# Attention and non-local block in one kernel: score blocks and value products in runs of six instead of four

## Chip, cores and metric

One Trainium2 chip, one core. The metric is the device time of one execution in microseconds (us), taken over several runs of each kernel. TensorE is the matmul engine, ScalarE applies functions (here the exponential) and copies, VectorE adds and inverts, GpSimd does a few multiplications. In the profile they are called PE (with PEld for its weight loads), ACT, DVE and POOL.

## The reference, cut to what matters

Eight images of 512 channels and 32 x 32 positions pass through an attention layer with eight heads of 64 channels, then through a non-local block and a normalization over the batch. All is fp32. The change touches only the middle three lines:

```
q, k, v = 1x1 convolutions of x          # (8, 8 heads, 64, 1024)
attn = softmax(einsum('bhdn,bhdm->bhnm', q, k) * 64**-0.5, axis=-1)
out  = einsum('bhnm,bhdm->bhdn', attn, v)
x    = x + conv1x1(out)
# theta, phi, g; f = theta phi^T / n; y = f g; z = conv1x1(y) + x; normalize z over the batch
```

## The kernel before

For one image the scores are cut into 64 blocks: 4 pairs of heads `p`, 2 halves `h` of the 1024 query positions, 8 stretches `m` of 128 key positions. A *score block* is the product of 128 keys with 512 queries for both heads of a pair (`ps`), which ScalarE turns into exponentials `e`. A *value product* multiplies `e` of one block with the values and adds it to `po`; eight of them make one *sum*, for one `(p, h)`. VectorE meanwhile adds the eight `e` to `acc`; the matrix product of ones and `acc` (`psum`, the *row-sum product*) gives the softmax's denominator, which VectorE inverts. TensorE writes scores with two heads as two row tiles (64*128) and value and row-sum products with two heads as two column tiles (128*64); going from one shape to the other costs time, and so the kernel works in runs: `RUN` score blocks, then `RUN` value products of the run before. In the code below, cuts are marked `...` and the comments are added.

```python
    RUN = 4
    ...
    w2 = ctx.enter_context(tc.tile_pool(name="w2", bufs=2))               # acc, ri
    ring = ctx.enter_context(tc.tile_pool(name="ring", bufs=12))          # e blocks
    psS = ctx.enter_context(tc.tile_pool(name="psS", bufs=1, space=PSUM)) # 3 tags x 2 banks: scores
    psO = ctx.enter_context(tc.tile_pool(name="psO", bufs=2, space=PSUM)) # 2 banks: po and psum
    ...
    def attention(b, q, k, v, before_last):
        o = mats.tile([P, CC, N], F32, tag="o", name=f"o_{b}")
        steps = [(p, h, m) for p in range(NPAIR) for h in range(NH) for m in range(NB)]
        runs = [steps[i:i + RUN] for i in range(0, len(steps), RUN)]
        ...
        def normalize(p, h, lead):
            s = slice(h * 512, (h + 1) * 512)
            ps = psO.tile([P, 512], F32, tag="o", name=f"psum_{b}_{p}_{h}")
            acc = accs.pop((p, h))
            columns(ps, lambda j: ones, lambda j: acc[:, j, :], True, True, lead)
            ri = w2.tile([P, 512], F32, tag="ri", name=f"ri_{b}_{p}_{h}")
            nc.vector.reciprocal(ri, ps)
            nc.vector.tensor_tensor(o[:, p, s], o[:, p, s], ri, ALU.mult)

        def weighted(run, due):
            lead = True
            if due:
                normalize(*due.pop(), True)
                lead = False
            for p, h, m in run:
                if m == 0:
                    sums[p, h] = psO.tile([P, 512], F32, tag="o", name=f"po_{b}_{p}_{h}")
                ps, e = sums[p, h], es.pop((p, h, m))
                columns(ps, lambda j: v[:, m, (2 * p + j) * D:(2 * p + j + 1) * D], lambda j: e[:, j, :],
                        m == 0, m == NB - 1, lead)
                lead = False
                if m == NB - 1:
                    nc.scalar.copy(o[:, p, h * 512:(h + 1) * 512], sums.pop((p, h)))
                    due.append((p, h))

        due = []
        for i, run in enumerate(runs):
            scores(run)
            if i:
                weighted(runs[i - 1], due)
        before_last()                  # q of the next image
        weighted(runs[-1], due)
        normalize(*due.pop(), False)
        return o
```

PSUM is the memory in which this kernel puts its matmul results, in tiles of one bank, 512 columns, or two. `po` and `psum` share the two banks of `psO`; six more banks (`psS`) hold scores. `columns` issues the two column tiles; its `lead` form splits the very first product of a value run. TensorE's order is the program's order.

## Time and profile before

| | before |
|---|---|
| median of 3 runs (us) | 2346.35 (2342.19 to 2347.3) |
| span of the profiled run (us), mean granted clock | 2342.2, 0.982 |
| busy share: TensorE, VectorE, ScalarE | 96%, 60%, 30% |
| value runs in an image | 16 |
| score run of 4 blocks, value run of 4 products, the same with a row-sum product (us) | 3.63, 3.59, 4.45 |

The last row is read from start to start: from the first matmul of one run to the first of the next. The main lines of this profile stand in the prediction below. TensorE's timeline at the end of the second image's attention (start, length, instruction, count), where the last row-sum product follows the last value products and the next image's value projection follows that:

```profile
543.60 2.75 PE L289 MATMUL po<-e,v 128*64 128x512 f32 x12
546.17 1.03 PE L289 MATMUL psum<-acc,ones 128*64 128x512 f32 x4
547.13 3.72 PE L171 MATMUL pv<-w_WvT,x 128*128 128x256 f32 x16
```

A length in this view reaches past the start of the next row (543.60 + 2.75 is 546.35, and the next row starts at 546.17); the starts count.

### The profile page before, as it was taken

To read this page: it belongs to the slowest core of one execution; us is meant where nothing else is said; L and a number is where in the kernel's file an instruction comes from. 1 tells how busy PE (TensorE), PEld (TensorE's weight loads), DVE (VectorE), ACT (ScalarE), POOL (GpSimd) and SP (SyncE) were. 2 spreads that over 40 slices of the span, in tenths; PEclk is the share of its full clock that TensorE was granted. 3 is DMA by queue.
4 is the path that set the end of the run, shared out by engine and by line. 5 is a ranking of instruction groups with operands and counts; after the bars stand their busy time and mean duration, and the time that the engine had idled before them with its cause. 6 is when DMAs were issued, how large, how long until landed. Compare 5 with 4: busy or idle time off the path is not lost.

```text
span 2342.2 us, 20797 instructions
## 1 busy us (share of the span) xinstructions
PE 2240.7 (96%) x8562; PEld 1127.6 (48%) x8562; DVE 1397.7 (60%) x1261; ACT 704.4 (30%) x819; POOL 61.7 (3%) x56
## 2 busy tenths in 40 slices
PE   4999999999999999999999999999999999999990
PEld 1533655336643466434563355633655346643360
DVE  2277445783567744687348854488445773477745
ACT  0155102541035310453104521154202541035205
POOL 2000110000000000000000000000000000000000
PEclk7999999999999999999999999999999999999995
DMA  6000122001130021200121002210113001200327
GB/s 233 1 1 7 64 85 108 28 1 63 47 135 1 1 76 66 104 1 32 48 94 72 1 32 76 90 48 1 63 47 135 1 1 63 79 16 1 108 86 310
DMA packets 30950, 141.94 MB, mean 61 GB/s; under 512 B 4096, under 2 KB 10496, under 8 KB 26112
## 3 DMA queue, kind: packets, MB, share of 16 engines
q1 hardware_dynamic: 26000, 131.87, 15.2%
q10 hardware_dynamic: 4848, 8.67, 1.0%
q8 instruction: 69, 1.13, 0.2%
q14 instruction: 33, 0.27, 0.0%
HBM read 101.07 MB, written 39.45 MB: 60 GB/s over the span
## 4 chain that ended last, share of the span: by engine, by line
PE 94%; ACT 2%; DVE 1%; DMA 1%; POOL 0%; issue 0%; ACTq 0%; DVEq 0%; POOLq 0%
PE ps L270 20%; PE po L289 17%; PE pv L171 8%; PE ptp L171 8%; PE pk L171 8%; PE pp L171 8%; PE pq L171 8%; PE pg L171 4%; PE pz L171 4%; PE pf L359 2%; PE psum L289 1%; PE pwf L378 1%; ACT z L504 1%; PE po L287 1%; PE po L286 1%; PE psum L287 1%
## 5 line engine op out<-in xcount | busy, mean ns | idle before, releaser
L273 ACT ACTIVATE e<-ps 128x1024 f32<-128x1024 f32 x512 | 482.5, 1030 | 360.3 <-PE ps L270 360.3
L279 DVE TENSOR_TENSOR acc<-acc,e 128x1024 f32<-128x1024 f32 x384 | 467.4, 1217 | 164.0 <-ACT e L273 135.7
L270 PE MATMUL ps<-q,k 64*128 64x512 f32 x2048 | 473.3, 603 | 1.6 <-POOL q L256 1.6
L289 PE MATMUL po<-e,v 128*64 128x512 f32 x1904 | 464.3, 594 | 0.0
L270 PEld LDWEIGHTS ps<-q,k 64*128 64x128 f32 x2048 | 187.6, 187 | 284.2 <-issue 233.6
L289 PEld LDWEIGHTS po<-e,v 128*64 128x64 f32 x1904 | 153.3, 137 | 211.9 <-issue 200.7
L297 DVE RECIPROCAL ri<-psum 128x512 f32<-128x512 f32 x64 | 214.5, 3352 | 10.2 <-PE psum L289 10.2
L368 ACT ACTIVATE g<-pg,gb 128x512 f32<-128x512 f32 x32 | 22.0, 687 | 428.6 <-PE pg L171 428.6
L171 PE MATMUL pq<-t_x,w_WqT 128*128 128x512 f32 x256 | 117.8, 608 | 26.0 <-ACT q L228 21.1
L188 DVE TENSOR_TENSOR k<-k,pk 128x1024 f32<-128x1024 f32 x24 | 29.3, 1221 | 163.1 <-PE pk L171 163.1
L171 PE MATMUL pp<-t_o,w_WpT 128*128 128x512 f32 x256 | 116.3, 602 | 1.9 <-DVE x L331 1.9
L171 PE MATMUL ptp<-w_tp,t_x 128*128 128x256 f32 x512 | 114.4, 379 | 0.0
L171 PE MATMUL pv<-w_WvT,t_x 128*128 128x256 f32 x512 | 114.4, 379 | 0.0
L171 PE MATMUL pk<-t_x,w_WkT 128*128 128x512 f32 x256 | 113.8, 592 | 0.0
L171 PEld LDWEIGHTS ptp<-w_tp,t_x 128*128 128x128 f32 x512 | 97.3, 190 | 13.2
L171 PEld LDWEIGHTS pv<-w_WvT,t_x 128*128 128x128 f32 x512 | 97.3, 190 | 13.2
L228 ACT ACTIVATE q<-pq,bq 128x512 f32<-128x512 f32 x64 | 40.4, 684 | 182.8 <-PE pq L171 182.8
L171 PE MATMUL pq<-x,w_WqT 128*128 128x512 f32 x192 | 88.7, 605 | 5.3 <-DMA w_WqT<-in_WqT_dram 5.3
L171 PEld LDWEIGHTS pq<-t_x,w_WqT 128*128 128x128 f32 x256 | 49.9, 196 | 90.1 <-issue 62.4
L188 DVE TENSOR_TENSOR q<-q,pq 128x1024 f32<-128x1024 f32 x24 | 29.3, 1221 | 102.1 <-PE pq L171 102.1
L277 DVE TENSOR_TENSOR acc<-e,e 128x1024 f32<-128x1024 f32 x64 | 78.3, 1223 | 16.6 <-ACT e L273 15.7
L171 PE MATMUL pp<-o,w_WpT 128*128 128x512 f32 x192 | 88.2, 603 | 0.0
(117 smaller groups left out, 2193.2 us busy)
## 6 DMA issues: line engine op xcount, KB each, us to landing
x<-in_x_dram SPq DMA_DIRECT2D x32, 512.0 KB, 5.5
w_WpT<-kept_WpT SPq DMA_DIRECT2D x7, 1792.0 KB, 7.1
w_tp<-kept_tp SPq DMA_DIRECT2D x7, 1792.0 KB, 7.2
spill<-x SPq DMA_DIRECT2D x24, 512.0 KB, 3.8
z<-spill SPq DMA_DIRECT2D x24, 512.0 KB, 8.4
out_dram<-z SPq DMA_DIRECT2D x24, 512.0 KB, 6.0
w_WqT<-kept_WqT SPq DMA_DIRECT2D x6, 1792.0 KB, 7.4
w_WvT<-kept_WvT SPq DMA_DIRECT2D x6, 1792.0 KB, 7.0
```

Of the source, the lines that this page charges most:

```text
L171: pe(nc.tensor.matmul(to_ps, lhsT(k), rhs(k), start=(s, at) not in begun, stop=(k == nk - 1), skip_group_check=True))
L188: nc.vector.tensor_tensor(at, at, ps, ALU.add)
L228: nc.scalar.activation(t[:, c, cols(q)], ps[:, m, :], AF.Identity, bias=bias[:, c:c + 1])
L270: pe(nc.tensor.matmul(ps[:, j, :], k[r, p, m * P:(m + 1) * P], q[r, p, h * 512:(h + 1) * 512], start=True, stop=True))
L273: nc.scalar.activation(e, ps, AF.Exp, scale=SCALE)
L277: nc.vector.tensor_tensor(accs[p, h], es[p, h, 0], e, ALU.add)
L279: nc.vector.tensor_tensor(accs[p, h], accs[p, h], e, ALU.add)
L286: pe(nc.tensor.matmul(to[:, :LEAD], l, r[:, :LEAD], start=start, stop=False, skip_group_check=True))
L287: pe(nc.tensor.matmul(to[:, LEAD:], l, r[:, LEAD:], start=False, stop=stop, skip_group_check=True))
L289: pe(nc.tensor.matmul(to, l, r, start=start, stop=stop, skip_group_check=True))
L297: nc.vector.reciprocal(ri, ps)
L359: pe(nc.tensor.matmul(ps[:, c, :], tp[:, i, c * P:(c + 1) * P], tp[:, i, CI:], start=(i == 0), stop=(i == NB - 1)))
```

## The change

Fewer changes between the two shapes: 11 value runs an image instead of 16. Twelve buffers for `e` hold exactly two runs of six.

```diff
-    RUN = 4
+    RUN = 6
```

## The prediction

> **What bounds the kernel now.** I read four views, in this order: the page (busy shares and chain), the groups by line, the timeline of single engines over the attention of the second image, and the waits of the matmul engine.
>
> The page first. The columns are busy time, share of the span and number of instructions; below it stands the chain that ended last.
>
> ```profile
> PE   2240.7 (96%) x8562; PEld 1127.6 (48%) x8562; DVE 1397.7 (60%) x1261; ACT 704.4 (30%) x819; POOL 61.7 (3%) x56
> ...
> PE 94%; ACT 2%; DVE 1%; DMA 1%; POOL 0%; issue 0%; ACTq 0%; DVEq 0%; POOLq 0%
> PE ps L270 20%; PE po L289 17%; PE pv L171 8%; PE ptp L171 8%; PE pk L171 8%; PE pp L171 8%; PE pq L171 8%; PE pg L171 4%; PE pz L171 4%; PE pf L359 2%; PE psum L289 1%; PE pwf L378 1%; ACT z L504 1%; PE po L287 1%; PE po L286 1%; PE psum L287 1%
> ```
>
> TensorE is the bound: it is on the chain for 94% of the span, and scores (L270) with value products (L286 to L289) are some 40% of it. Nothing else comes near, so a change counts only by the time in which TensorE issues no matmul, or issues one late. The groups (busy us, mean ns, then idle before) give the companions of one score block:
>
> ```profile
> L273 ACT ACTIVATE e<-ps 128x1024 f32<-128x1024 f32 x512 | 482.5, 1030 | 360.3 <-PE ps L270 360.3
> L279 DVE TENSOR_TENSOR acc<-acc,e 128x1024 f32<-128x1024 f32 x384 | 467.4, 1217 | 164.0 <-ACT e L273 135.7
> L297 DVE RECIPROCAL ri<-psum 128x512 f32<-128x512 f32 x64 | 214.5, 3352 | 10.2 <-PE psum L289 10.2
> ```
>
> The timeline, TensorE and ScalarE rows of one run of four score blocks and one of four value products (start, length, instruction):
>
> ```profile
> 411.29 3.70 PE L270 MATMUL ps<-q,k 64*128 64x512 f32 x16
> ...
> 414.93 0.32 PE L286 MATMUL po<-e,v 128*64 128x128 f32 x1
> ...
> 415.84 2.75 PE L289 MATMUL po<-e,v 128*64 128x512 f32 x12
> ...
> 418.52 1.56 PE L270 MATMUL ps<-q,k 64*128 64x512 f32 x6
> 418.63 0.59 ACT L313 COPY o<-po 128x512 f32<-128x512 f32 x1 [2.39 <-PE po L289]
> ```
>
> The reader is to see that one period of scores and values (411.29 to 418.52) is 7.23 us without any idle entry on PE, and that the copy of a finished `po` (ScalarE, L313) runs beside the next scores, so it costs nothing. The first score run holds two runs back to back:
>
> ```profile
> 400.63 7.14 PE L270 MATMUL ps<-q,k 64*128 64x512 f32 x32
> ```
>
> It lasts 7.07 us from its start to the first value product at 407.70; 16 matmul records last 3.64 us (411.29 to 414.93). So 16 more records cost 3.43 us, 0.86 us a block, and entering the run costs 3.64 - 3.43 = 0.21. A value run takes 418.52 - 414.93 = 3.59 us for the same 3.43 of work: 0.16 for entering. **One pair of changes costs 0.21 + 0.16, or 7.23 - 6.87 = about 0.355 us** with the unrounded starts. The waits of the matmul engine in the whole kernel show no wait inside attention, but one wait of the kind that matters below, TensorE for a ScalarE copy that it follows at once:
>
> ```profile
> PE pz L171 <- ACT wf L380: 9.3, 8, 1.2
> ```
>
> **What the Trainium skill says.** "TensorEngine Tiling (Array Packing)", Key Properties: changing the tiling mode, not just the tile, drains TensorE. The trace agrees: score records (64*128) and value records (128*64) start in pairs 0.43 us apart, and 0.53 us across each change. It is what the change wants to save. "PSUM — Partial Sum Buffer", the section on bank collisions: TensorE may not write a bank that another engine reads, and the semaphores must see to it; so a new `po` in a bank must wait until the copy or the reciprocal that reads it has ended. The trace before shows no collision and no such wait in attention. "TensorE: Matmul & The Clock Gate", the table at its head: ScalarE takes its queue strictly in order; so a copy also waits for the exponentials ahead of it. The copy above ran 0.11 us after the next scores began, with the exponentials long done. "Perfetto Trace Analysis", Tensor Engine Instruction: a matmul's end is estimated, not observed; I therefore count from start to start.
>
> **The change part by part.** One image has 4 head pairs x 2 halves x 8 = 64 blocks: 16 runs of four before, now ten of six and one of four. No instruction for a block is added or removed; the built order shows that only the 80 TensorE rows of the split lead products go.
>
> *Removed.* Value runs per image go from 16 to 11, so 5 pairs of changes go: 5 x 0.355 = 1.78 us an image, x 8 images = **-14.2 us**. All on the path, because TensorE is.
>
> *Moved: the products of the sums.* Before, a sum of eight products (`po`) always ended a run; its bank was copied out while four score blocks ran, and the row-sum product `psum` opened the next value run in the other of the two banks. With six, eight does not divide: sums end inside runs 1, 2, 5, 6 and 9 (counted from 0) and the next sum begins at once. It needs a bank. In runs 1, 5 and 9 the other bank is free (a reciprocal has read it; see below). But runs 2 and 6 open with a `psum`, which has taken the other bank, so the next `po` must take the bank of the `po` that ended one instruction earlier, and waits for its copy. The built program says so: the first product of po_1_0 and po_2_1 carries a wait on ScalarE, and both have the bank of the sum before. A third such wait stands at the end: the `psum` of the seventh sum has slipped behind the next image's q projection, into the last value run, and so the eighth `psum` gets the bank of the eighth `po`, just ended, with a wait on ScalarE. In the kernel before, none of the `po` products and no `psum` had a wait on ScalarE.
>
> *Cost of one such wait.* From the trace: the last pair of `po` starts at 417.99 and the copy at 418.63, 0.64 later; it takes 0.59; `pz` after the `wf` copy starts 0.05 after the copy's end. Without the wait the next pair would start 0.43 after the last. The restart after an empty array costs a further 0.10 (0.53 instead of 0.43, as at a change of mode). 0.64 + 0.59 + 0.05 - 0.43 + 0.10 = 0.95 us. Three an image, eight images: 3 x 8 x 0.95 = **+22.8 us**.
>
> *Added: twelve score blocks at the start.* ScalarE needs 0.92 us a block when busy (the 8 at 401.87 took 7.44: (7.44 - 1.03) / 7), TensorE 0.86, and three score buffers lie between. In the eight blocks of before, weights for the last block were loaded some 0.25 us ahead of its matmul; that lead shrinks by 0.06 a block, so the 12th block comes some 0.1 to 0.2 us late: 8 x 0.15 = **+1.2 us**. Runs of six begin with ScalarE idle and stay clear of it.
>
> *VectorE beside it.* With `psum` later by up to a run, the first addition into an `acc` buffer waits for the `psum` that reads its old content (two buffers), and reciprocals come later. I laid out one image by hand with 1.3 us an addition (3.88 us for three in the timeline) and 4.0 us for a reciprocal with its multiplication: VectorE idles twice (some 10 and 7 us), but ends each piece before TensorE needs it; the tightest are the banks of the third and sixth `psum`, read by the reciprocal 4 to 6 us before a `po` takes them, and the data sums of the next image, ready 2 to 3 us before use. Twelve block buffers hold exactly two runs of six; each is free 4 us or more before its exponential. So VectorE adds nothing by this count.
>
> Sum: -14.2 + 22.8 + 1.2 = **+9.8 us**, 2346.35 + 9.8 = **2356 us**.
>
> **The rivals.** (a) *Only the changes go.* If the waits for the copies were hidden (the copy starts earlier, or the matmul queue bridges them), the time would be 2346 - 14 = 2332. For: the changes are measured, 0.355 a pair. Against: nothing stands in TensorE's order between the last product and the next one into the same bank. I give it one in ten. (b) *VectorE becomes the bound.* It has 56 x 1.3 + 8 x 4 = 105 us in an image's attention of some 118 us, and now idles in the middle. If my hand layout is out by more than the 4 us of slack, a `po` waits for a reciprocal (3.35 us) once or twice an image: +8 x 2 to 5 = 2372 to 2396. For: 89% load and two long idle times. Against: each reciprocal starts as soon as its `psum` is there. One in ten. (c) *The end of the image suffers*: the seventh and eighth reciprocal now both follow the q projection, and the products of `o` must be ready for the output projection. Against: the value projection of 25 us lies between, except in the last image: at most +3 us.
>
> **Range and chances.** The three runs before spread over 5 us; the cost of a wait may be 0.7 to 1.1 us, which moves the sum by -6 to +4; rival (b) stretches the top, rival (a) the bottom. Range 2342 to 2368. A change of 2% is 47 us, more than any rival but the end of (b): faster 0.01, same 0.96, slower 0.03.
>
> **What would show it.** Right: TensorE's waits list `po` waiting for the ScalarE copy of L313, 16 times at about 0.65 to 0.9 us, and `psum` 8 times; six-block runs last 5.35 us of scores and 5.3 us of values, 80 changes fewer. Wrong: `po` waiting for the reciprocal (b), no wait at all (a), scores waiting for exponentials in runs of six, or q or v projections that start late. A time under 2342 would mean that the copies are hidden; one over 2368 that VectorE or the buffers of the blocks hold TensorE up.

## The result, and the profile after

| | before | after |
|---|---|---|
| median of 6 runs (us) | 2343.26 (2341.89 to 2347.3) | 2352.43 (2349.68 to 2353.0) |
| ratio to before, 95% interval | 1 | 1.0034 (1.0021 to 1.0047) |
| span of the profiled run (us), mean granted clock | 2342.2, 0.982 | 2350.8, 0.981 |
| all score runs, 8 images (us) | 465.0 | 458.7 |
| all value and row-sum runs, 8 images (us) | 514.7 | 529.2 |

A ratio here and below is the mean time of one kernel's fast runs over that of the other's of the same rounds, so it is not quite the ratio of the medians quoted. The last two rows add up, from matmul starts in the trace, the time from the first matmul of each run to the first of the next run. They contain every wait in it. The change lost 8.6 us in the traces, and these two stages account for 14.5 - 6.3 = 8.2 of them.

TensorE has less to do and takes longer. Its busy line on the page after:

```profile
PE 2234.9 (95%) x8482; PEld 1118.1 (48%) x8482; DVE 1388.8 (59%) x1261; ACT 699.8 (30%) x819; POOL 61.7 (3%) x56
```

Eighty matmul records and 5.8 us of busy time are gone, and yet the span grew. What TensorE waited for (us in total, times, longest):

```profile
PE po L289 <- ACT o L313: 10.9, 16, 0.7
PE pz L171 <- ACT wf L380: 9.3, 8, 1.2
PE psum L289 <- ACT o L313: 4.8, 7, 0.7
```

The line in the middle was there before. The first and third are new: value products and row-sum products that wait for the copy of a finished sum. TensorE's timeline of the value run in which it happens first in the second image:

```profile
434.57 0.32 PE L286 MATMUL psum<-acc,ones 128*64 128x128 f32 x1
...
435.48 3.60 PE L289 MATMUL po<-e,v 128*64 128x512 f32 x16
439.77 1.94 PE L289 MATMUL po<-e,v 128*64 128x512 f32 x8 [0.68 <-ACT o L313]
441.64 1.56 PE L270 MATMUL ps<-q,k 64*128 64x512 f32 x6
```

The run opens with the row-sum product of the first sum (L286), ends the second sum (16 records are four blocks), and the third sum begins at 439.77 only, after 0.68 us without a matmul. In the same run of the kernel before, this place did not exist: a sum ended a run. The chain of work that ended last shows that the copy itself lies on the path (start, length, what):

```profile
435.65 3.46 PE po L289 x16
439.11 0.02 issue
439.13 0.59 ACT o L313
439.73 0.04 issue
439.77 1.94 PE po L289 x8
```

The idle time understates the loss, because the modelled length of the last matmul reaches into the gap: eight pairs from 435.48, 0.43 apart, put the start of the last pair at 438.49, and the next pair starts 1.28 later, 0.85 more than usual. From start to start, this run took 441.64 - 434.57 = 7.07 us; a run of six with a row-sum product and no wait takes 6.17. So one wait cost **0.90 us**: these 0.85, and 0.05 by which the pair after that was late. The place at the end of the image, to be held against the fence of before:

```profile
544.87 3.60 PE L289 MATMUL po<-e,v 128*64 128x512 f32 x16
549.16 1.08 PE L289 MATMUL psum<-acc,ones 128*64 128x512 f32 x4 [0.68 <-ACT o L313]
550.17 3.72 PE L171 MATMUL pv<-w_WvT,x 128*128 128x256 f32 x16
```

And the first stretch of scores, twelve blocks, with weight loads of its last blocks (PEld) that wait for an exponential:

```profile
402.55 10.77 PE L270 MATMUL ps<-q,k 64*128 64x512 f32 x48
```

```profile
409.44 0.30 PEld L270 LDWEIGHTS ps<-q,k 64*128 64x128 f32 x4 [0.59 <-ACT e L273]
...
412.19 0.30 PEld L270 LDWEIGHTS ps<-q,k 64*128 64x128 f32 x4 [0.61 <-ACT e L273]
```

From 402.55 to the first value product at 413.25 are 10.70 us; twelve blocks at 0.859 and 0.21 for entering would be 10.52. It lost 0.18 us, in each of images two to eight. The four loads from 409.44 to 412.19 are 0.92 us apart, the pace of ScalarE and not the 0.86 of TensorE.

VectorE changed most to the eye. These are its groups and waits with the most idle time before them; `acc<-e,e` is the first addition into an `acc` buffer:

```profile
L279 DVE TENSOR_TENSOR acc<-acc,e 128x1024 f32<-128x1024 f32 x384 | 467.1, 1216 | 36.4 <-ACT e L273 8.3
...
L277 DVE TENSOR_TENSOR acc<-e,e 128x1024 f32<-128x1024 f32 x64 | 78.1, 1220 | 151.7 <-PE psum L289 136.8
```

It now waits 136.8 us for row-sum products (in the kernel before, this line idled 16.6 us, of which 15.7 for exponentials), since a buffer of `acc` is free only when its row-sum product has read it. VectorE in the run of the first wait shown above:

```profile
435.77 1.23 DVE L277 TENSOR_TENSOR acc<-e,e 128x1024 f32<-128x1024 f32 x1 [9.76 <-PE psum L289]
436.91 3.35 DVE L297 RECIPROCAL ri<-psum 128x512 f32<-128x512 f32 x1
```

The reciprocal follows the addition that waited for the same row-sum product, and ends at 440.26, after TensorE has gone on at 439.77 in the bank of the finished sum. No TensorE wait names VectorE in attention, so this waiting has not reached the path; experiment e7 tests that.

### The profile page after: what moved, and what is told of

It is laid out like the page before. It is cut to its first block, busy times and chain, and to the rows that moved or that the text cites. A ratio compares the mean times of both kernels' runs of the same rounds, so it can differ in the third digit from the quotient of the medians.

```text
span 2350.8 us, 20693 instructions
## 1 busy us (share of the span) xinstructions
PE 2234.9 (95%) x8482; PEld 1118.1 (48%) x8482; DVE 1388.8 (59%) x1261; ACT 699.8 (30%) x819; POOL 61.7 (3%) x56
## 4 chain that ended last, share of the span: by engine, by line
PE 94%; ACT 2%; DVE 1%; DMA 1%; POOL 1%; issue 0%; ACTq 0%; DVEq 0%; POOLq 0%
PE ps L270 20%; PE po L289 18%; PE pv L171 8%; PE ptp L171 8%; PE pk L171 8%; PE pp L171 8%; PE pq L171 8%; PE pg L171 4%; PE pz L171 4%; PE pf L359 2%; PE psum L289 1%; PE pwf L378 1%; ACT z L504 1%; PE psum L287 1%; PE psum L286 1%; ACT o L313 1%
## 5 line engine op out<-in xcount | busy, mean ns | idle before, releaser
L289 PE MATMUL po<-e,v 128*64 128x512 f32 x1984 | 459.5, 594 | 10.9 <-ACT o L313 10.9
L270 PE MATMUL ps<-q,k 64*128 64x512 f32 x2048 | 464.3, 600 | 1.6 <-POOL q L256 1.6
L277 DVE TENSOR_TENSOR acc<-e,e 128x1024 f32<-128x1024 f32 x64 | 78.1, 1220 | 151.7 <-PE psum L289 136.8
L313 ACT COPY o<-po 128x512 f32<-128x512 f32 x64 | 37.4, 585 | 171.5 <-PE po L289 171.5
```

The source lines that it names most:

```text
L270: pe(nc.tensor.matmul(ps[:, j, :], k[r, p, m * P:(m + 1) * P], q[r, p, h * 512:(h + 1) * 512], start=True, stop=True))
L277: nc.vector.tensor_tensor(accs[p, h], es[p, h, 0], e, ALU.add)
L289: pe(nc.tensor.matmul(to, l, r, start=start, stop=stop, skip_group_check=True))
```

## The experiments

The theory: the kernel pays for 23 waits for the copy of a finished sum, 0.90 us each, because with six a sum ends inside a run, and a row-sum product at the head of the run holds the other bank. The rivals: the runs of six are dear in themselves (the twelve score blocks, VectorE's late additions and reciprocals), or the changes of shape were worth less than thought. Each kernel gave the right result.

### e1: the row-sum product in the run where its sum ends

```diff
 # the changed kernel, in weighted(), after the loop over the run
+            if due and run[-1][2] != NB - 1:
+                normalize(*due.pop(), False)
```

> Runs of six as in the changed kernel, but where a sum of eight ends inside a run its row-sum product is issued at the end of that same run instead of at the start of the next one, so no product needs the bank of a sum that has just ended. Theory (24 waits for the ScalarE copy of a finished sum, 0.90 us each, ate the 14.2 us that the 40 removed pairs of mode changes save): no wait of po or psum for the copy on TensorE; the time falls by 24 x 0.90 = 21.6 us against the changed kernel, to about 2331 us, ratio to the kernel before about 0.9946. Rival (the first score run of twelve, or the later additions and reciprocals of VectorE, are what makes runs of six dear): the waits go but the time stays at or above the kernel before, 2343 to 2352 us.

Measured: **2331.67 us** (2330.34 to 2333.24, 5 runs), before 2344.48, ratio 0.9943 (0.993 to 0.9957). No wait of `po` or `psum` for a copy is left on TensorE. Its timeline, one value run of six:

```profile
433.44 0.32 PE L286 MATMUL po<-e,v 128*64 128x128 f32 x1
...
434.36 4.46 PE L289 MATMUL po<-e,v 128*64 128x512 f32 x20
438.65 1.03 PE L289 MATMUL psum<-acc,ones 128*64 128x512 f32 x4
439.61 5.42 PE L270 MATMUL ps<-q,k 64*128 64x512 f32 x24
```

The sum ends inside the `x20` row, the next begins without a gap, and the row-sum product comes last, in the bank of the sum that ended two blocks earlier and has been copied meanwhile. The run takes 439.61 - 433.44 = 6.17 us. All value runs together fall to 508.4 us, 20.8 under the changed kernel (23 x 0.90 = 20.7), and score runs stay at 458.7. The same number of runs of six, without the waits: the rival of the twelve score blocks is out, and the saving of 14.2 us that the change was made for is there. The edit also lets VectorE wait less for row-sum products (92.9 us instead of 136.8); that VectorE was not what cost is left to e7.

### e2: one such wait put into the kernel before

```diff
 # the kernel before, RUN = 4, in weighted()
-            if due:
-                normalize(*due.pop(), True)
+            if due and run is not runs[-2]:
+                normalize(*due.pop(0), True)
```

> The kernel before with runs of four, in which only the row-sum product of the seventh sum is held back to the last value run, so that the eighth row-sum product gets the bank of the sum just ended, once an image. Nothing else of runs of six is in it. Theory: psum waits for the ScalarE copy 8 times, about 0.68 us of idle time each in the waits, 0.9 us from start to start: +7.2 us, about 2350.5 us, ratio 1.0031. Rival (such a wait is not what costs): ratio within 0.001 of 1.

Measured: 2349.75 us (2348.15 to 2350.61), before 2344.48, ratio 1.0019 (1.0005 to 1.0033). TensorE's waits:

```profile
PE psum L289 <- ACT o L313: 4.8, 7, 0.7
```

Seven waits, not eight: in the last image no q projection stands between the last two value runs, and the eighth row-sum product follows the reciprocal of the seventh instead, as it does in the kernel before. All value runs rose from 514.7 to 521.1, by 6.4 us, or 0.91 a wait; score runs are unchanged (465.3). The timed difference, some 4.5 us by the ratio, is smaller than both, but its interval holds 6.4 (1.0027). So the wait alone, with no run of six anywhere, costs what it cost in the changed kernel.

### e3: runs of two

```diff
-    RUN = 4
+    RUN = 2
```

> The kernel before with runs of two: 32 value runs an image instead of 16, still dividing eight, so no bank wait. It doubles the suspected saving with the sign turned: 16 more pairs of mode changes an image x 8 x 0.355 us = +45 us, about 2389 us, ratio 1.0194. If a pair cost only half of that in truth (and the change had less to gain than thought), +23 us, ratio 1.010.

Measured: 2392.46 us (2392.2 to 2392.72), ratio 1.0203 (1.0187 to 1.0219). Its timeline, two score blocks and two value products:

```profile
435.10 1.99 PE L270 MATMUL ps<-q,k 64*128 64x512 f32 x8
437.02 0.32 PE L286 MATMUL po<-e,v 128*64 128x128 f32 x1
...
437.93 1.03 PE L289 MATMUL po<-e,v 128*64 128x512 f32 x4
438.89 1.99 PE L270 MATMUL ps<-q,k 64*128 64x512 f32 x8
```

The period is 438.89 - 435.10 = 3.79 us for 4 x 0.859 = 3.44 of work: 0.35 for a pair of changes. Over the whole kernel 128 pairs more took 46.5 us more in the two stages (490.9 + 535.3 against 465.0 + 514.7), 0.363 a pair. The saving was sized rightly. TensorE's waits show none for a copy here.

### e7: runs of six that divide the sums better

```diff
 # the changed kernel, in attention()
-        runs = [steps[i:i + RUN] for i in range(0, len(steps), RUN)]
+        runs, at = [], 0
+        for n in (6, 6, 4) * 3 + (4,) * 4:
+            runs.append(steps[at:at + n])
+            at += n
```

> Runs of 6, 6, 4 three times and then 4, 4, 4, 4: 13 value runs an image; most runs are of six and the first score run has twelve blocks as in the changed kernel, but no run both opens with a row-sum product and begins a new sum in its middle. Theory: no wait for the copy; 3 pairs of changes fewer an image, 3 x 8 x 0.355 = -8.5 us, and +1.4 us for the twelve score blocks at the start: about 2336 us, ratio 0.997. Rival (runs of six are dear in themselves): at or above the kernel before, ratio 1.000 to 1.003.

Measured: 2340.08 us (2337.08 to 2340.78), ratio 0.9974 (0.9961 to 0.9988). There is no wait for a copy; score runs take 461.9 us, value runs 511.0, together 6.8 under the kernel before. A line of VectorE's waits:

```profile
DVE acc L280 <- PE psum L292: 129.0, 23, 8.0
```

VectorE waits here nearly as long for row-sum products as in the changed kernel (136.8), and the kernel is faster than before. Its idling did no harm here.

### e4 and e5: the copy of a finished sum made twice

```diff
 # e4: in the changed kernel; e5: in the kernel before
+                    nc.scalar.copy(o[:, p, h * 512:(h + 1) * 512], sums[p, h])
                     nc.scalar.copy(o[:, p, h * 512:(h + 1) * 512], sums.pop((p, h)))
```

In e4 the build answered with another choice of banks: two sums an image now take the bank of the row-sum product that opened their run.

> The changed kernel with each finished sum copied out twice by ScalarE, one copy after the other. The built program answers by another choice of banks: po_1_0 and po_2_1 now take the bank of the row-sum product that opened their run, so they wait for its reciprocal on VectorE instead of for the copy; only the eighth row-sum product still waits for the (now two) copies. Theory (what counts is when the last reader of the bank ends): in the changed kernel's trace the reciprocal ends 0.54 us after TensorE resumed behind the copy, so 16 waits lose 1.44 us instead of 0.90, and 7 lose some 0.59 more: 16 x 0.54 + 7 x 0.55 = +12.5 us against the changed kernel, about 2365 us, ratio to the kernel before 1.009. Rival (the waits lie beside other losses): same as the changed kernel, 1.0034.

Measured: 2365.44 us (2362.58 to 2366.75), ratio 1.009 (1.0074 to 1.0105), as expected. It was run on another chip. TensorE's waits:

```profile
PE po L289 <- DVE ri L297: 21.5, 16, 1.7
...
PE psum L289 <- ACT o L314: 9.1, 7, 1.3
```

The first kind is now a wait for the reciprocal. TensorE and VectorE in the run where it happens first in the second image:

```profile
436.47 0.32 PE L286 MATMUL psum<-acc,ones 128*64 128x128 f32 x1
...
442.31 1.94 PE L289 MATMUL po<-e,v 128*64 128x512 f32 x8 [1.32 <-DVE ri L297]
444.18 1.13 PE L270 MATMUL ps<-q,k 64*128 64x512 f32 x4
```

```profile
437.67 1.22 DVE L277 TENSOR_TENSOR acc<-e,e 128x1024 f32<-128x1024 f32 x1 [9.76 <-PE psum L289]
438.81 3.35 DVE L297 RECIPROCAL ri<-psum 128x512 f32<-128x512 f32 x1
```

VectorE makes the addition that waited for the row-sum product first, and the reciprocal only then. Such a run takes 444.18 - 436.47 = 7.71 us from start to start, 1.54 over the 6.17 without a wait, where the copy had cost 0.90; expected were 1.44. TensorE goes on 0.15 us after the reciprocal's end at 442.16, where it had followed the copy by 0.05. The loss followed the end of the bank's last reader.

> The kernel before with each finished sum copied out twice, as in e4. Here the copies run beside the next scores and no product needs the bank at once. Theory: 64 more copies of 0.59 us, 37 us of ScalarE time, cost nothing: ratio 1.000 within 0.001. Rival (ScalarE time itself counts, through the exponentials behind the copy): up to +10 us, ratio 1.004.

Measured: 2343.53 us (2342.74 to 2346.29), before 2342.81, ratio 1.0004 (0.9988 to 1.0019). It was run on another chip. Sixty-four copies more on ScalarE leave the score runs (465.2) and value runs (514.8) as they were. A copy was free here where no product needed its bank at once.

### e6: ten score blocks at the start instead of twelve

```diff
 # e1, in attention()
-        runs = [steps[i:i + RUN] for i in range(0, len(steps), RUN)]
+        runs = [steps[:4]] + [steps[i:i + RUN] for i in range(4, len(steps), RUN)]
```

> As e1 (runs of six, each row-sum product in the run where its sum ends), but the first run has four blocks and the rest six, still 11 runs an image: the first stretch of scores has ten blocks instead of twelve. Theory (from the eighth block on, each score block waits some 0.06 us more for ScalarE): of the 0.18 us that twelve blocks lose an image, about 0.12 are won back, 8 x 0.12 = 1 us, about 2330.5 us, ratio to the kernel before 0.994; no wait of po or psum for a copy. Rival: the first stretch loses as much with ten as with twelve, or the longer last run of six holds up the next image; then at or above e1.

Measured: 2331.13 us (2330.5 to 2331.47), before 2342.81, ratio 0.9947 (0.9933 to 0.996). It was run on another chip. Not told apart from e1 by time, each by its ratio to the kernel before. In the trace the first stretch of the second image takes 8.87 us for ten blocks (10 x 0.859 + 0.21 = 8.80), so it loses 0.07 instead of 0.18. All score runs of an image take 57.03 us in images two to eight, against 57.14 in e1: the 0.11 is won there each time, 0.8 us in seven images. But in the first image the first stretch takes 11.82 us for ten blocks (12.24 for twelve in e1), which hides it in the sum over eight images (score runs 459.2, in e1 458.7); that stretch differs by a microsecond and more from run to run. Whether the whole kernel gains stays open.

**The best version** is e1 (or e6, which is the same by time): 13 us, or 0.6%, under the kernel before, and 0.9% under the changed kernel by the ratios.

## Why the prediction was right

*Size.* 2356 us predicted, 2352.43 measured; +9.8 us predicted, +8.0 by the ratio (0.0034 of 2343) and +8.6 in the traces. Of the 3.6 us between 2356 and 2352.43, 3.1 are the starting point: the prediction counted from the median of three runs before, 2346.35, and that of six is 2343.26. In its parts: -14.2, + 20.7 for the waits and + 1.4 for the twelve blocks make 7.9, and the two stages show 8.2.

*Pairs of changes: -14.2.* Right. In the after trace runs of six took 5.35 and 5.31 us as predicted. e3 found 0.363 us a pair against 0.355, and e1, in which nothing stands against the saving but the twelve blocks, 12.6 us less in the two stages (6.3 in each), where -14.2 + 1.4 would give -12.8.

*Waits for the copy: +22.8.* The mechanism is shown three ways: by the trace after, by taking the waits away (e1), by putting one in (e2). The size was a little high in both factors. 0.95 us a wait was predicted, 0.90 measured; 24 waits were counted, 23 came. I had read the waits of the first images from the built order and assumed the eighth image to be like them; in it nothing comes between the last two value runs, and its last row-sum product follows the reciprocal of the seventh sum instead of a copy. This reciprocal ends at 2207.39 and the product starts at 2207.45, only some 0.2 us late, and the kernel before has the same small wait at this place. In the cost of one wait, the start of the copy (0.64), its length (0.59) and the 0.05 behind it came as predicted; the restart was set at 0.10, taken from a change of shape, and measured 0.05. 23 x 0.90 = 20.7 instead of 22.8: that is 2.1 us of overshoot.

*Twelve score blocks: +1.2.* 0.18 us in the second image, so about 8 x 0.18 = 1.4. The working behind 0.15 is loose: 0.25 us of lead less four times 0.06 is about nothing, and does not give a delay by itself. In the trace after, the last loads come at the pace of ScalarE, and three steps of 0.06 are the 0.18. e6 shows the same lag shrink to 0.07 with ten blocks, in the trace only.

*VectorE: nothing.* Right: two idle times of 9.76 and 8.43 us in the second image (10 and 7 predicted), and no wait for VectorE on TensorE in attention but the 0.2 us in the last image; e7 has 129 us of such idling and gains.

*The rivals.* (a), the copies are hidden, fell with the first wait line of the trace after. (b), VectorE becomes the bound, did not happen; e4 shows what it would have cost had the banks been chosen the other way round: 1.54 us a wait instead of 0.90, at two places an image. VectorE need not be the bound for that: a choice of bank that the source leaves to the build decides which of the two engines TensorE waits for. The ground given against (b), that each reciprocal starts as soon as its `psum` is there, was wrong: at 435.77 VectorE first made an addition, and the reciprocal began at 436.91. That (b) stayed away is due to the banks, which had been read from the built program, and not to this ground. (c), the end of the image, had only the `psum` wait that was counted.

## What to carry to other kernels

When a run length no longer divides the length of an accumulation, ask which bank the next accumulation gets and who reads it last: a copy that ran for free beside other work comes onto the path the moment its bank is needed by the next instruction. Here the cure was to move an instruction, not to undo the change: a product that needs a second bank belongs where the other bank's copy has had time to end. Such a wait can be read before any run from the semaphore waits and banks of the built program, and sized from the old trace: last start to reader's start, plus the reader's length, plus the restart (0.05 us here), less the normal spacing.

## What the Trainium skill lacked or had wrong

- "TensorEngine Tiling (Array Packing)", Key Properties, says that a change of tiling mode drains TensorE, but not what that costs. Here pairs of matmul records start 0.43 us apart within a run and 0.53 across a change; a pair of changes, with the split first value product, costs 0.355 us in the kernel before and 0.363 on average over the 128 more of e3.
- "PSUM — Partial Sum Buffer", the section on bank collisions, says that an access must be guarded, but not what the turn of a bank costs. Here TensorE lost 0.90 us where the next product needed a bank that ScalarE copied out in 0.59, and 1.54 us where it needed one whose reciprocal (3.35 us) was still running.
- No page that I read says that an allocation of banks with the same source text elsewhere can change with a neighbouring instruction; in e4 one more copy on ScalarE made the build give two sums an image the other bank, and turned 0.90 us a wait into 1.54.
